# Decoder layer (scan, attention, experts) on one core: whole scan steps, unpadded queries and keys, maxima by one transpose

## The chip, the core and the metric

The kernel runs on one core of a Trainium2 chip. A core has five instruction queues that run beside each other: TensorE (PE: matrix products, with its own weight loads), VectorE (DVE), ScalarE (ACT), GpSimd (POOL) and SyncE (SP), which here issues every DMA. Each queue works in order, and an instruction that must wait holds up what stands behind it. Matrix products write to PSUM, which the kernel uses as eight banks of 512 numbers for each of 128 partitions; everything else lies in SBUF. The metric is the device time of one execution in microseconds; lower is better.

## The reference

32 sequences of 256 tokens and width 256 go through three blocks, each followed by a residual sum and a layer norm. All numbers are fp32.

```python
# 1: a selective scan (d_inner 512, 16 states), restarted every 64 tokens
xc, res = split(x @ W_in.T + b_in);  u = silu(causal_conv3(xc))
dlt, Bm, Cm = split(u @ W_x.T);      delta = softplus(dlt @ W_dt.T + b_dt)
carry = exp(delta * A) * carry + delta * Bm * u;   y = sum_n(carry * Cm)
x = layernorm(x + (y * silu(res)) @ W_out.T + b_out)
# 2: cross attention to ctx, 16 heads of 16
x = layernorm(x + softmax(q k^T / 4) v @ w_o.T + b_o)
# 3: 8 experts by position (32 tokens of each sequence), FF 704
x = layernorm(x + (silu(x w1) * (x w3)) w2)
```

## The kernel before

Everything is one program for 32 batches. The work is written as chains, Python generators that say which engine they need next and when they can go on; `in_order` always advances the chain that can start earliest (a chain's lag shifts its rank among those that want the same engine). The times that it goes by are constants in the source: `MM` for a matrix product, `EV`, `VE`, `GP` for evictions, 4.5 us (`LANDING`) for a DMA from issue to landing, and nothing for the issue itself. The order so found is fixed in the program; on the chip every queue keeps it.

The chains that matter here, with their lines in the profile:

- `pre(b)` (lines 346 to 466) projects the input, convolves, and makes `delta`, `u` and their product. It writes them to DRAM, and `load_step` (479) reads them back, spread over partitions, for one of 16 scan steps of a batch (two DMAs of 256 KB, four buffers).
- `decays` (506) makes the factors `da` of a step by four exponentials on ScalarE. `scan` (527) takes a step in two halves of 512 columns: a product `bu` into PSUM (L544), and the scan `h` (L563), both on VectorE. `weighted` (575) multiplies `h` by C on POOL (L580), and `sums` (583) adds over states on TensorE (L594) for four steps at a time, which frees four of the six buffers of `h`.
- `mixes` (651) is the output product, the residual and the layer norm of the scan block.
- `keys(b)` (619) projects keys and values of a batch. `attn(b)` (689) projects queries; both are written with each head padded from 16 to 32 rows, so that four heads fill 128 partitions (two products of two blocks each, L327). Scores are computed twice. First with queries on partitions (L715): VectorE takes each head's maximum (L731) into `mpad`, eight 128 x 128 transposes bring the maxima into the padding rows of the queries' layout (L739), and VectorE subtracts the result from `qT` (L742); a padding row of ones in `kT` does the rest. Then with keys on partitions: ScalarE takes the exponential of each head (L775), and TensorE multiplies by the values (L751). Scores always go by groups of four heads on four 32-row parts of TensorE, with a PSUM bank for each head.
- `finish(b)` (800) divides, projects and normalizes; it stores the result as `x2d`.
- `expert_unit` (947) takes one expert for two groups of four sequences; these units fill in between and remain at the end.

PSUM holds one bank for `bu`, one for `b_bc` (B spread over partitions) and a ring of six (`RING`) that all other products share through `take(n, rank, t)`, the lowest rank first. `keys`, `attn` and the next `keys` follow each other, since there is one set of keys and values; the scan of later batches runs beside them. All DMAs stand in SP's queue in the order of the chains. A DMA there also waits for the eighth one before it, since eight completion semaphores are used in turn.

Of the kernel before, what the change touches and what calls it, by code (L numbers as in the profile page):

```python
# [8 lines left out]
F32 = mybir.dt.float32  # L9
AF = mybir.ActivationFunctionType  # L10
ALU = mybir.AluOpType
# [19 lines left out]
RING = 6  # L31
# [64 lines left out]
def decoder_kernel(ctx: ExitStack, tc: tile.TileContext, a: dict, out: bass.AP):  # L96
# [58 lines left out]

    w_in = weight("w_in", D, 2 * DI)
# [29 lines left out]
    w_k = weight("w_k", D, NG * P)  # L186
    b_k = column("b_k", NG)
    w_v = weight("w_v", D, D)
    w_out = weight("w_out", DI, D)
    w_q = weight("w_q", D, NG * P)  # L190
    b_q = column("b_q", NG)
# [58 lines left out]
    mpad = keep.tile([P, 2, NG, P], F32, name="mpad")  # L250
    nc.gpsimd.memset(mpad, 0.0)
# [18 lines left out]

    def done(n, t):
        free.extend(n * [t])
# [13 lines left out]
    MM = 0.43  # L286
# [51 lines left out]
    xs_at, xps, dds, sress, bcds, ygs, spread, silus = {}, {}, {}, {}, {}, {}, {}, []  # L338
# [7 lines left out]
    def pre(b):  # L346
# [51 lines left out]
        u = unit1.tile([P, NDC, L], F32, tag="u", name=f"u_{b}")  # L398
        for c2 in range(2):
            t = biased(u, AF.Silu, conv_b, pss[c2], c2)  # L400
            done(1, t)
        nc.scalar.activation(sres, sres, AF.Silu)
# [4 lines left out]
        exps()  # L407
        yield from take(1, 3, t)
# [36 lines left out]
        for h in range(2):  # L445
            cc = slice(2 * h, 2 * h + 2)

            lost = unit1.tile([P, 2, L], F32, tag="xT", name=f"lost_{b}")
            nc.gpsimd.tensor_scalar(lost, e[:, cc], 1.0, -1.0, op0=ALU.add, op1=ALU.add)
            nc.gpsimd.tensor_tensor(lost, e[:, cc], lost, ALU.subtract)  # L450
            nc.gpsimd.tensor_tensor(z[:, cc], z[:, cc], lost, ALU.add)
            yield spend("POOL", 3 * GP[2]), "POOL" if h == 0 else "ACT"
# [13 lines left out]
        spread[b] = t + 3.0  # L466

    def pres():
        for b in range(B):
            yield from pre(b)  # L470
        while silus:
            silus.pop(0)()
# [54 lines left out]
    def scan():  # L527
# [4 lines left out]
        for i in range(STEPS):  # L532
            b, k = divmod(i, NBLK)
            if i + AHEAD < STEPS:
                yield lambda: spread.get((i + AHEAD) // NBLK), "SP"
                load_step(i + AHEAD)
            yield max(lds_at[i], b_bcs[b][1], recurred.get(i - 1, 0.0) - 0.3 - MARGIN), "DVE"
            b_bc = b_bcs[b][0]
            for g in range(GB):

                if g:
                    yield t - 0.3 - MARGIN, "DVE"
                bu = ps_bu.tile([P, NQ, L], F32, tag="bu", name="bu")
                nc.vector.tensor_tensor(  # L544
                    bu, loads[i][:, 1, g].unsqueeze(1).to_broadcast([P, NQ, L]), b_bc, ALU.mult
                )
                t = spend("DVE", 0.66)
                if g == GB - 1:
                    del loads[i]
                    if k == NBLK - 1 and b + 1 < B:  # L550
                        yield t, "PE"
                        spread_b(b + 1)
                t -= 0.3 + MARGIN
                if g == 0:
                    yield lambda: (
                        max(t, decayed[i], min(h_free)) if i in decayed and h_free else None
                    ), "DVE"
                    h_free.sort()
                    del h_free[0]
                    h = hs[i] = hp.tile([P, GB, NQ, L], F32, tag="h", name="h")  # L560
                else:
                    yield t, "DVE"
                nc.vector.tensor_tensor_scan(  # L563
                    h[:, g].rearrange("p q t -> p (q t)"),
                    das_of[i][:, g].rearrange("p q t -> p (q t)"),
                    bu.rearrange("p q t -> p (q t)"),
                    0.0,
                    op0=ALU.mult,
                    op1=ALU.add,
                )  # L570
                t = spend("DVE", 1.17)
            del das_of[i]
            recurred[i] = t
# [9 lines left out]
    def sums():  # L583


        for i in range(NJ - 1, STEPS, NJ):
# [16 lines left out]
            t = spend("PE", GB * NQ * MM + 0.3)  # L603
# [14 lines left out]

    def keys():

        for b in range(B):
# [4 lines left out]
            kT = unit1.tile([P, NG, L], F32, tag="kT", name=f"kT_{b}")  # L626
            for g2 in range(2):
                yield from take(1, 4, t0)
                ps, t = product(
                    "ps_qk",  # L630
                    lambda j: [
                        w_k[:, k, (2 * g2 + j) * P : (2 * g2 + j + 1) * P] for k in range(2)
                    ],
                    lambda j: [ctxT[:, k, :] for k in range(2)],
                )
                yield t, "ACT"
                t = biased(kT, AF.Identity, b_k, ps, g2)
                done(1, t)
# [10 lines left out]
            kts[b] = kT, t  # L649
# [39 lines left out]
    def attn(b):  # L689
# [3 lines left out]
        qT = unit1.tile([P, NG, L], F32, tag="qT", name=f"qT_{b}")  # L693
        for g2 in range(2):
            yield from take(1, 2, tx)
            ps, t = product(
                "ps_qk",
                lambda j: [w_q[:, k, (2 * g2 + j) * P : (2 * g2 + j + 1) * P] for k in range(2)],
# [471 lines left out]
```

## Time and profile before

| | |
|---|---|
| median of 3 runs | 3283.39 us (3279.27 to 3285.63) |
| profiled execution | 3283.71 us, span 3282.0 us, granted clock 0.897 |
| TensorE busy | 2697.9 us (82%) |
| VectorE busy | 2584.0 us (79%) |
| ScalarE, POOL busy | 1970.8 us (60%), 1857.3 us (57%) |
| DMA, mean | 139 GB/s, 47.8% of the engines' time |
| scan steps | 512, from 119 us on |

A group row of the profile names the line, the engine, the operation, output and inputs, shapes and count; behind the bar stand the busy time and the mean duration in ns, and then how long the engine had been idle before such instructions, with the instruction that ended most of it. An fp32 matrix product counts twice there, as two passes. A timeline row gives start and duration in us and how many instructions were merged; a window row gives the busy time of each engine in one stretch. SP's rows are issues of DMAs; they are not counted as busy.

### The profile page before, as it was taken

What the parts mean: (1) busy time and instruction counts of PE and PEld (TensorE: products, weight loads), DVE (VectorE), ACT (ScalarE), POOL (GpSimd) and SP (SyncE); (2) the same over time, 40 slices, a digit from 0 to 9 for tenths busy, and PEclk for the clock granted to TensorE, in tenths of its full rate; (3) what the DMA queues carried; (4) which work ended last, traced back from release to release, by engine and by line L of the source; (5) the groups of instructions that cost most, each with busy time, mean ns of one, the idle gap of its engine ahead of it and who ended that gap; (6) DMA issues with size and microseconds to landing.
All of it is one profiled execution on the core that took longest, in us unless ns stands there. A gap on an engine that the chain in (4) does not pass through costs nothing.

```text
span 3282.0 us, 52502 instructions
## 1 busy us (share of the span) xinstructions
PE 2697.9 (82%) x18436; PEld 1907.2 (58%) x18436; DVE 2584.0 (79%) x3511; ACT 1970.8 (60%) x4211; POOL 1857.3 (57%) x1241
## 2 busy tenths in 40 slices
PE   2568787878888988888888898888788888898987
PEld 1345555556556666566555566556566556565776
DVE  0598989898988988888989878989878898884211
ACT  0556666666666766676666656766656666764411
POOL 1576666666766656665656556665656666642000
PEclk9678888888889899999998899899899889899998
DMA  3354444444445555444544544445445544454474
GB/s 89 110 149 115 139 120 138 126 138 127 132 129 151 158 145 147 140 134 133 154 137 138 145 140 147 137 137 140 128 142 148 148 139 137 130 152 132 130 225 140
DMA packets 310681, 455.00 MB, mean 139 GB/s; under 512 B 37969, under 2 KB 158033, under 8 KB 310417
## 3 DMA queue, kind: packets, MB, share of 16 engines
q1 hardware_dynamic: 310416, 451.64, 47.8%
q8 instruction: 146, 2.39, 0.3%
q14 instruction: 119, 0.97, 0.1%
HBM read 400.67 MB, written 50.86 MB: 138 GB/s over the span
## 4 chain that ended last, share of the span: by engine, by line
DVE 44%; PE 27%; POOL 8%; ACT 8%; DMA 6%; issue 5%; SPq 2%; DVEq 1%; ACTq 0%; POOLq 0%
DVE h L563 23%; DVE bu L544 12%; PE ps_h L978 7%; PE s L715 4%; DVE mpad L731 4%; POOL h L580 3%; PE ps_down L1058 3%; PE ps_in L327 3%; PE y L594 3%; PE ps_oT L751 2%; ACT da L519 2%; ACT es L775 2%; PE ps_conv L327 2%; DMA ld<-dd 1%; PE ps_qk L327 1%
## 5 line engine op out<-in xcount | busy, mean ns | idle before, releaser
L580 POOL TENSOR_TENSOR h<-h,c_bc 128x1024 f32<-128x1024 f32 x512 | 1207.8, 2360 | 935.0 <-DVE h L563 810.8
L563 DVE TENSOR_TENSOR_SCAN h<-da,bu 128x512 f32<-128x512 f32 x1024 | 1248.4, 1219 | 116.8 <-PE y L594 11.0
L519 ACT ACTIVATE da<-ld,a_neg 128x252 f32<-128x252 f32 x2048 | 889.9, 506 | 395.6 <-DVE h L563 289.8
L544 DVE TENSOR_TENSOR bu<-ld,b_bc 128x512 f32<-128x512 f32 x1024 | 709.6, 693 | 95.4 <-PE b_bc L503 68.1
L594 PE MATMUL y<-h,sel_y 128*32 128x256 f32 x4096 | 334.1, 440 | 85.6 <-POOL h L580 73.4
L731 DVE TENSOR_REDUCE mpad<-s 128x2 f32<-128x512 f32 x512 | 315.5, 681 | 111.3 <-PE s L715 110.8
L775 ACT ACTIVATE es<-s 128x512 f32<-128x512 f32 x512 | 263.9, 601 | 191.6 <-PE ps_oT L751 144.9
L978 PE MATMUL ps_h<-x2T,w 128*128 128x256 f32 (+3 forms) x1440 | 331.0, 377 | 41.3 <-ACT x2T L966 36.2
L715 PE MATMUL s<-kT,qT 32*128 32x256 f32 x2048 | 248.9, 475 | 101.9 <-DVE mpad L731 63.3
L978 PEld LDWEIGHTS ps_h<-x2T,w 128*128 128x128 f32 (+1 forms) x1440 | 241.5, 193 | 110.7 <-ACT x2T L966 40.3
L594 PEld LDWEIGHTS y<-h,sel_y 128*32 128x32 f32 x4096 | 150.3, 124 | 253.8 <-POOL h L580 119.6
L327 PE MATMUL ps_in<-xT,w_in 128*128 128x256 f32 x1024 | 268.9, 415 | 13.5 <-ACT xT L352 12.0
L715 PEld LDWEIGHTS s<-kT,qT 32*128 32x128 f32 x2048 | 155.4, 218 | 189.2 <-DVE mpad L731 98.8
L327 PEld LDWEIGHTS ps_in<-xT,w_in 128*128 128x128 f32 x1024 | 205.5, 208 | 68.9 <-issue 12.8
L715 PE MATMUL s<-qT,kT 32*128 32x256 f32 x2048 | 180.1, 438 | 39.4 <-DVE qT L742 23.4
L301 POOL TENSOR_SCALAR ln_rstd<-ln_mv 128x2 f32<-128x2 f32 x96 | 22.0, 230 | 309.6 <-DVE ln_mv L298 305.0
L327 PE MATMUL ps_conv<-xpad,taps 128*128 128x256 f32 x768 | 182.6, 388 | 0.0
L751 PE MATMUL ps_oT<-es,v 128*32 128x256 f32 x2048 | 149.1, 410 | 40.6 <-DVE h L1040 13.1
L1058 PE MATMUL ps_down<-w,h 128*128 128x256 f32 (+1 forms) x624 | 164.2, 409 | 16.4 <-DVE h L1040 7.5
L715 PEld LDWEIGHTS s<-qT,kT 32*128 32x128 f32 x2048 | 112.4, 202 | 96.1 <-issue 25.6
L327 PEld LDWEIGHTS ps_conv<-xpad,taps 128*128 128x128 f32 x768 | 146.5, 194 | 25.0 <-issue 3.1
L327 PE MATMUL ps_out<-w_out,yg 128*128 128x256 f32 x512 | 133.2, 419 | 28.5 <-ACT es L775 20.9
(124 smaller groups left out, 3701.4 us busy)
## 6 DMA issues: line engine op xcount, KB each, us to landing
ld<-dd SPq DMA_DIRECT2D x1024, 256.0 KB
w<-in_w SPq DMA_DIRECT2D x120, 352.0 KB
x<-in_x SPq DMA_DIRECT2D x64, 256.0 KB
dd<-delta SPq DMA_DIRECT2D x32, 512.0 KB
dd<-u SPq DMA_DIRECT2D x32, 512.0 KB
w13y<-in_w SPq DMA_DIRECT2D x40, 352.0 KB
w<-in_w SPq DMA_DIRECT2D x30, 384.0 KB
ctxT<-in_ctxT SPq DMA_DIRECT2D x32, 256.0 KB
```

Of the source, the lines that this page charges most:

```text
L327: nc.tensor.matmul(ps[:, j, :], l, r, start=(k == 0), stop=(k == len(terms) - 1))
L519: nc.scalar.activation(da[:, g, q].rearrange("p (k t) -> p k t", t=CHUNK)[:, :, 1:], loads[i][:, 0, g].rearrange("p (k t) -> p k t", t=CHU ...
L544: nc.vector.tensor_tensor(bu, loads[i][:, 1, g].unsqueeze(1).to_broadcast([P, NQ, L]), b_bc, ALU.mult)
L563: nc.vector.tensor_tensor_scan(h[:, g].rearrange("p q t -> p (q t)"), das_of[i][:, g].rearrange("p q t -> p (q t)"), bu.rearrange("p q t - ...
L580: nc.gpsimd.tensor_tensor(hs[i], hs[i], c_bc, ALU.mult)
L594: nc.tensor.matmul(y[32 * j : 32 * j + 32, :], sel_y[:, g, :], hs[i - NJ + 1 + j][:, g, q, :], start=(g == 0 and q == 0), stop=(g == GB - ...
L715: nc.tensor.matmul(ss[j][:, t, :], left[r : r + 32, g, t * P : (t + 1) * P], right[r : r + 32, g, :], start=True, stop=True,)
L731: nc.vector.tensor_reduce(mpad[:, :, g, 32 * j + DK], s, AX.X, ALU.max)
L751: nc.tensor.matmul(oT[32 * j : 32 * j + 32, :], v[:, k, 4 * g + j, :], ess[j][:, k, :], start=(k == 0), stop=(k == 1), tile_position=(0, 3 ...
L775: nc.scalar.activation(es, s, AF.Exp, scale=1.0 / DK**0.5)
L978: nc.tensor.matmul(ps[:m, i, :], w_tiles[u, which, e][k][:, f * P : f * P + m], right, start=(k == 0), stop=(k == 1),)
L1058: nc.tensor.matmul(po[:, j, :], h[i // m_in][:m, i % m_in, cols], w_tiles[u, "w2", e][f // 3][:m, f % 3, :], start=(i == terms[0]), stop=( ...
```

## The change

- A scan step is one product of 1024 columns into two PSUM banks and one scan of 1024. The ring of shared banks falls from six to five.
- Queries and keys are projected without padding: one product of two blocks instead of two. Each is evicted to a flat tile, from which 16 DMAs bring the heads to the old places (32 rows apart) in `qT` and `kT`, which are now fixed tiles. `kT` is set to one once. The weights are packed while loading (two DMAs each, pieces of 64 bytes), the biases by 16 DMAs each.
- Maxima are gathered in `tops`, 32 columns; one transpose makes 32 rows of them, ScalarE copies these with the sign turned, and 32 DMAs of one row each write them into the 17th row of each head in `qT`. The second scores contract 17 rows, the first 16.
- Scores go by two heads, or by four where `more` finds two further banks free.
- `u` has two buffers, and the second half of `pre` is a chain of its own (`sizes`, `steps`); `lost` works on quarters; the value of `MM` and some of the planner's constants change.

```diff
-RING = 6
+RING = 5
...
+    def heads(n):
+        w = wp.tile([P, 2, D], F32, name="w_" + n)
+        src = a["w_" + n].rearrange("(k p) (h c) -> p k h c", p=P, c=32)
+        for k in range(2):
+            dst = w[:, k].rearrange("p (h c) -> p h c", c=DK)
+            nc.sync.dma_start(dst, src[:, k, :, :DK])
...
+            nc.sync.dma_start(bias[r : r + DK, h // 8 : h // 8 + 1], src)
...
-    mpad = keep.tile([P, 2, NG, P], F32, name="mpad")
-    nc.gpsimd.memset(mpad, 0.0)
+    kT = keep.tile([P, NG, L], F32, name="kT")
+    nc.gpsimd.memset(kT, 1.0)
+    qT = keep.tile([P, NG, L], F32, name="qT")
+    tops = keep.tile([P, 2, H], F32, name="tops")
...
+    def more(n):
+        if sum(t <= clock.now for t in free) < n or len(asking) > 1 and min(asking) < 2:
+            return 0
+        free.sort()
+        del free[:n]
+        return n
...
-    MM = 0.43
+    MM = 0.47
...
-        u = unit1.tile([P, NDC, L], F32, tag="u", name=f"u_{b}")
+        u = unit2.tile([P, NDC, L], F32, tag="u", name=f"u_{b}")
...
-        for h in range(2):
-            cc = slice(2 * h, 2 * h + 2)
-            lost = unit1.tile([P, 2, L], F32, tag="xT", name=f"lost_{b}")
...
+        for c in range(NDC):
+            lost = unit1.tile([P, L], F32, tag="lost", name=f"lost_{b}")
...
-            for g in range(GB):
...
-                bu = ps_bu.tile([P, NQ, L], F32, tag="bu", name="bu")
...
+            bu = ps_bu.tile([P, GB, NQ, L], F32, tag="bu", name="bu")
+            nc.vector.tensor_tensor(
+                bu,
+                loads[i][:, 1].unsqueeze(2).to_broadcast([P, GB, NQ, L]),
+                b_bc.unsqueeze(1).to_broadcast([P, GB, NQ, L]),
+                ALU.mult,
+            )
...
+            nc.vector.tensor_tensor_scan(
+                h.rearrange("p g q t -> p (g q t)"),
+                das_of.pop(i).rearrange("p g q t -> p (g q t)"),
+                bu.rearrange("p g q t -> p (g q t)"),
+                0.0, op0=ALU.mult, op1=ALU.add,
+            )
...
+    def spread_heads(dst, flat):
+        for g in range(NG):
+            for j in range(4):
+                h = 4 * g + j
+                r = DK * (h % 8)
+                nc.sync.dma_start(dst[32 * j : 32 * j + DK, g, :], flat[r : r + DK, h // 8, :])
...
-        for g in range(NG):
-            yield from take(4, 2, tq)
-            ss, ts = scores(g, qT, kT)
-            for j, s in enumerate(ss):
+        h = 0
+        while h < H:
+            yield from take(2, 2, tq)
+            n = 2 + more(2 if h % 4 == 0 else 0)
+            ss, ts = scores(range(h, h + n), qT, kT, DK)
+            for s in ss:
                 yield ts, "DVE"
-                nc.vector.tensor_reduce(mpad[:, :, g, 32 * j + DK], s, AX.X, ALU.max)
+                nc.vector.tensor_reduce(tops[:, :, h], s, AX.X, ALU.max)
...
-                    nc.tensor.transpose(ps[:, j, n, :], mpad[:, n, 2 * g2 + j, :], ident)
...
-            nc.vector.tensor_tensor(q2, q2, ps.rearrange("p j t n -> p j (t n)"), ALU.subtract)
...
+        ps = bank("ps_m")[: 2 * H, :P]
+        nc.tensor.transpose(ps, tops.rearrange("p t h -> p (t h)"), ident)
...
+        nc.scalar.activation(rows, ps, AF.Identity, scale=-1.0)
...
+        for t in range(2):
+            for g in range(NG):
+                for j in range(4):
+                    h = t * H + 4 * g + j
+                    r = 32 * j + DK
+                    nc.sync.dma_start(qT[r : r + 1, g, t * P : (t + 1) * P], rows[h : h + 1, :])
+        tq = clock.now + LANDING
```

## The prediction

> **What bounds the kernel now.** I read the page's shares first, then the windows by stage, then single rows of the timeline. One execution took 3283.7 us around a span of 3282.0; the median of the runs shown is 3283.4, so sums against the span need 1.7 us more.
>
> ```profile
> PE 2697.9 (82%) x18436; PEld 1907.2 (58%) x18436; DVE 2584.0 (79%) x3511; ACT 1970.8 (60%) x4211; POOL 1857.3 (57%) x1241
> ...
> 0.00:120.00 120.00, 41.17 (x162) 34.05 (x163) 4.99 (x25) 22.90 (x41) 22.36 (x34) 0.93 0.32 86
> ...
> 1500.00:2100.00 600.00, 512.01 (x3628) 356.92 (x3621) 521.34 (x699) 398.85 (x864) 373.38 (x240) 0.91 0.49 139
> ...
> 3000.00:3282.00 282.00, 248.59 (x1524) 200.37 (x1524) 61.03 (x135) 77.24 (x143) 19.00 (x53) 0.93 0.50 156
> ```
>
> Each window row gives the stretch and its length, then the busy time of TensorE, its weight loads, VectorE, ScalarE and POOL, the granted clock and the DMA's share. In the middle stage TensorE works 512 of 600 us and VectorE 521. With some 0.1 us between neighbours on VectorE (699 instructions) that is 95% of the stage: VectorE sets the pace, TensorE stands close behind. The first scores of batch 0 start at 212 us, those of batch 31 at 3025: 90.7 us a batch. TensorE idles 3282 - 2698 = 584 us, of it 79 before 120 us and 33 after 3000. The granted clock is 0.91 to 0.93 whether TensorE is busy a third of the stretch (the start) or nearly nine tenths (the end), so I reckon with no change of it.
>
> ```profile
> L563 DVE TENSOR_TENSOR_SCAN h<-da,bu 128x512 f32<-128x512 f32 x1024 | 1248.4, 1219 | 116.8 <-PE y L594 11.0
> L544 DVE TENSOR_TENSOR bu<-ld,b_bc 128x512 f32<-128x512 f32 x1024 | 709.6, 693 | 95.4 <-PE b_bc L503 68.1
> ...
> L742 DVE TENSOR_TENSOR qT<-qT,ps_m 128x512 f32<-128x512 f32 x64 | 41.9, 674 | 5.1 <-PE ps_m L739 5.0
> L739 PE MATMUL ps_m<-ident,mpad 128*128 128x128 f32 x256 | 45.2, 302 | 22.0 <-DVE mpad L731 22.0
> L327 PE MATMUL ps_qk<-x1T,w_q 128*128 128x256 f32 x512 | 126.1, 391 | 0.0
> L327 PE MATMUL ps_qk<-ctxT,w_k 128*128 128x256 f32 x512 | 125.3, 389 | 7.2 <-DMA ctxT<-in_ctxT 4.7 <-DVE yg L610 2.5
> ...
> 1524.97 1.15 PE L715 MATMUL s<-qT,kT 32*128 32x256 f32 x16
> ```
>
> These are the work that changes: scan and product, the subtraction and transposes of the maxima, the projections, and (last line) one group of scores, four heads in 1.15 us.
>
> The resource that the page hardly shows is SP's queue:
>
> ```profile
> 7.89 40.98 SPq L181 DMA_DIRECT2D a_neg<-in_a_log  x64
> ...
> 50.44 0.26 ACT L183 ACTIVATE a_neg<-a_neg 128x64 f32<-128x64 f32 x1 [48.37 <-DMA a_neg<-in_a_log]
> ...
> L422 SPq DMA_DIRECT2D bcd<-xp x32: 335/524/1106, 91.8 to 2836.6; - x32
> L485 SPq DMA_DIRECT2D ld<-dd x1024: 513/554/1889, 111.6 to 2962.7; - x171
> ```
>
> Whatever its size (16 rows in L422, 256 KB in L485), an issue holds SP about 0.54 us; 64 tiny ones took 0.64 each. The last of these ended at 48.87 and ScalarE, which needed it, started at 50.44: 1.6 us to landing.
>
> **The change, part by part.**
>
> Whole scan steps. L1040's product with a PSUM operand takes 413 ns for 256 elements and 687 for 512: 274 per 256, 139 fixed. So 1024 cost 1.235 us instead of 2 x 0.693. The scan shows one size: 2.30 if its fixed part is the same 139, 2.44 if nothing is fixed; I take 2.30. In an undisturbed stretch a half step recurs every 2.07 us (product starts at 118.99, 121.07, 123.12), so 0.16 of it is gaps, then paid once. A step falls from 4.13 to 3.69 us: 225 us over 512 steps (154 with the dearer scan). The subtraction's 42 us go too. VectorE has 267 us less, 8.3 a batch. That is no gain unless TensorE can follow.
>
> TensorE's work. The projections halve: -126. One transpose of 32 columns a batch for eight: -45 + 32 x 0.3 = -36. Scores: the built program holds 77 groups of four heads and 358 of two where there were 256 of four, because the ring has five banks. 16 passes on four row groups are four slots (1.15 us); two heads are eight passes on two row groups, again four slots. So 179 groups are added at about 1.0 us (some overlap with neighbours): +179. Bounds: 0 if two heads cost half, +206 at the full 1.15. Work after: 2698 - 126 - 36 + 179 = 2715. The saved padding is spent again.
> The Trainium skill ("TensorEngine Tiling (Array Packing)", Key Properties) says that a change of tiling mode drains TensorE, which speaks against more, smaller groups; in the trace the weight load at 1521.24, after scores, shows 0.33 us of "issue" before it. By the rule, 179 groups x 2 changes x 0.33 would be an estimated 118 us more.
>
> The maxima's new path. Before, VectorE subtracted them. Now: transpose, a ScalarE copy of 128 columns (between 0.26 for 64 columns in L183 and 0.47 for 256 in L416: 0.35), then 32 SP issues of one row each, ordered by half and then by head. The first score group needs both halves of its heads, hence the 17th issue: 0.1 + 0.35 + 0.1 + 17 x 0.54 + 1.6 = 11.3 us (8.4 at 0.37 each, the low end of L422; 18 if 20 issues at 0.64 are needed and landing takes the 4.7 us of the longest wait of L519 for a load). The planner adds 4.5 us and nothing for SP. In the built order the first score group follows the transpose directly in 19 of 32 batches; the others have 0.7 to 5 us between, 28 in all. What is queued behind: sums of y, on which the release of four of six h buffers hangs, so VectorE runs dry after two more steps (7.4 us). Dead time: 32 x 11.3 - 28 = 334 (241 to 548). The same place cost 22.0 (L739) + 23.4 (first scores after L742) = 45.
>
> Spreading queries and keys: 16 issues each. Their first group needs four: 4 x 0.54 + 1.6 = 3.8 us, and between projection and scores most batches have 10 to 25 us of TensorE work. I cost it at nothing on TensorE; without that cover it is 32 x 3.8 = 122.
>
> SP's total: 64 issues x 0.54 = 35 us more a batch, beside some 55 x 0.54 = 30 us. It fits in 90, but loads stand behind bursts. Four load buffers are four steps, 14.8 us; a burst of 32 plus landing plus the exponentials (1.7) is 20.6. VectorE can run dry for 5.8 us; that falls in the same dead stretch, so I don't add it (+186 if it did not).
>
> Start: 34 more issues stand before the first load of x, 17 to 22 us, and the queries' and keys' weights now come in 64-byte pieces: 8192 against 128 pieces in each of the 64 small transfers at 0.64 us, up to 41. I take +30 (17 to 60).
>
> Two buffers of u and separate size computation, `lost` in quarters (12 instructions for 6), 4 fewer ScalarE evictions: POOL and ScalarE are 57% and 60% busy. Nothing, bounded by 20 us either way.
>
> Sum, on TensorE's queue: work 2715; idle at the start 79 + 30, at the end 33; dead 334; and the remaining waits. Before, these were 584 - 79 - 33 - 45 = 427, of which waits for POOL's h are 86 (L594), b_bc 38 and scores for reductions 102 (L715): upstream engines get ahead during the dead time, so I drop them and keep 200. The bounds are 0 and 427; the bank that the ring loses works towards the upper one, since scores, sums and projections all wait for banks, and the wait of scores for reductions (102) is the row that it would lengthen. 2715 + 109 + 33 + 334 + 200 = 3391, and 1.7 around it: **3393 us**, 3.3% slower.
> Another rule of the skill, to coalesce many small transfers ("DMA: Bandwidth & Descriptors", Rules for kernel authors), speaks against 64 pieces a batch too; that page puts a fixed 2.0 us on a transfer, which for the 1.6 measured here would give an estimated 13 us more.
>
> **Rivals.**
> Faster: the other waits collapse, since all that stands behind the dead stretch is ready when it ends, and VectorE's 267 us count. The break-even is remaining waits under 92 us (183 if the dead stretch is the short 8.4). With 0 to 92: 3191 to 3283; I name 3200. For: TensorE's waits are mostly on VectorE and POOL. Against: waits inside attention (L751 41, L978 41, L327 after exponentials 28) don't depend on the scan.
> Much slower: late loads and dead stretches don't coincide, and the waits remain: 3393 + 186 = 3579. For: in 12 late batches 43 to 46 issues stand between two load steps (25 us). Against: there the scan waits for its buffers anyhow.
> The change does what its words say: two-head groups are cheap (half): 3393 - 179 = 3214. The four slots of 1.15 us speak against it.
>
> **Numbers.** Slower as summed 0.55, much slower 0.16, faster by waits or cheap groups 0.26, unchanged 0.03. The runs spread by 0.2% (3279.3 to 3285.6), which is what can be told from no change. The range reaches into the faster cases down to 3190 and the slow one up to 3600; the likeliest case's own is 3300 to 3500.
>
> **What would show it.** Right: in nearly every batch TensorE idles 9 to 14 us between the transpose of maxima and the next scores, released by a DMA; about 435 score groups; a scan row near 2.30 us, a product near 1.24; VectorE's share falls below 75%. Wrong: row issues well under 0.4 us, TensorE above 82% busy, or the scores' busy time not rising.

## The result

The changed kernel takes 4075.1 us (median, 4064.6 to 4080.6), the kernel before 3282.8 in the same runs: a ratio of 1.241, with a 95% interval of 1.238 to 1.244. The prediction was 3393 (3190 to 3600). The sign is right, and the loss is seven times as large: 792 us, not 110. The profiled execution has a span of 4069.2 us and 1.7 us around it.

The lines of the page after that answer to those shown of before: shares by engine, granted clock, the chain that ended last by engine, then the groups (busy time and mean ns behind the bar, then idle time ahead of them and who ended it).

```profile
PE 3015.8 (74%) x17700; PEld 2056.3 (51%) x17700; DVE 2404.7 (59%) x2423; ACT 1937.1 (48%) x4135; POOL 1888.8 (46%) x1433
...
PEclk9777877777778877778878777887777887778878
...
PE 38%; SPq 18%; DVE 14%; DMA 11%; ACT 8%; issue 6%; POOL 4%; DVEq 0%; ACTq 0%; POOLq 0%
...
L592 DVE TENSOR_TENSOR_SCAN h<-da,bu 128x1024 f32<-128x1024 f32 x512 | 1169.2, 2284 | 121.1 <-PE y L621 65.0
L554 ACT ACTIVATE da<-ld,a_neg 128x252 f32<-128x252 f32 x2048 | 863.3, 499 | 762.9 <-DMA ld<-dd 488.9
L576 DVE TENSOR_TENSOR bu<-ld,b_bc 128x1024 f32<-128x1024 f32 x512 | 627.0, 1225 | 201.2 <-DMA ld<-dd 107.0
L751 PE MATMUL s<-qT,kT 17*128 17x256 f32 x2048 | 394.4, 541 | 411.6 <-DMA qT<-rows 368.6
```

The rows of before that answer to the second, the third and (from the list of waits) the fifth of these lines:

```profile
PEclk9678888888889899999998899899899889899998
...
DVE 44%; PE 27%; POOL 8%; ACT 8%; DMA 6%; issue 5%; SPq 2%; DVEq 1%; ACTq 0%; POOLq 0%
```

```profile
ACT da L519 <- DMA ld<-dd: 97.1, 71, 4.7
```

After the change no engine is busy for more than three quarters of the span. The chain held 44% VectorE and 2% SyncE's queue before; now SyncE's queue is 18% of it. ScalarE's wait for the loads of the scan steps, 97 us before, is 489. TensorE's wait for the rows of maxima is 369, close to what was predicted. The granted clock fell from 0.897 to 0.793: TensorE's 318 us of extra busy time are about the same work at a slower clock (by the span's mean clock, 2698 x 0.897 = 2420 us at full clock before, 3016 x 0.793 = 2392 after).

By stage: the first scan starts at 139 us instead of 120, the last one at 3621 instead of 2982, and from there to the end it takes 448 us instead of 300. So 620 of the 787 us that the span grew lie in the scan stage (108.8 us a batch, before 89.4), 148 in the tail and 19 at the start.

What happens in the scan stage shows in 30 us of the timeline (start, duration, queue, instruction; in brackets the idle time before it and its releaser):

```profile
1432.59 0.39 PE L774 MATMUL ps_m<-ident,tops 128*32 128x128 f32 x1 [3.10 <-DVE tops L768]
...
1433.73 1.16 SPq L520 DMA_DIRECT2D ld<-dd  x2
...
1434.98 20.54 SPq L786 DMA_DIRECT2D qT<-rows  x32
...
1437.45 2.29 DVE L592 TENSOR_TENSOR_SCAN h<-da,bu 128x1024 f32<-128x1024 f32 x1
...
1441.13 2.29 DVE L592 TENSOR_TENSOR_SCAN h<-da,bu 128x1024 f32<-128x1024 f32 x1
...
1446.90 3.89 PE L751 MATMUL s<-qT,kT 17*128 17x256 f32 x16 [13.92 <-DMA qT<-rows]
...
1454.50 0.42 DVE L637 TENSOR_TENSOR yg<-y,sres 128x256 f32<-128x256 f32 x1 [11.08 <-PE y L621]
...
1455.62 5.35 SPq L520 DMA_DIRECT2D ld<-dd  x8
...
1456.20 2.29 DVE L592 TENSOR_TENSOR_SCAN h<-da,bu 128x1024 f32<-128x1024 f32 x1
...
1458.94 1.69 ACT L554 ACTIVATE da<-ld,a_neg 128x252 f32<-128x252 f32 x4 [6.87 <-DMA ld<-dd]
```

SyncE issues 32 rows from 1434.98 to 1455.52. TensorE waits 13.9 us for them, with the sum of y behind the scores in its queue, and VectorE for that sum. But the loads of the next scan steps stand in SyncE's queue behind the same 32 issues: the first goes out at 1455.62 and ScalarE can use it at 1458.94. Two waits end at nearly the same time.

### The profile page after: what moved, and what is told of

Its sections match the earlier page's. It is cut to its first block, busy times and chain, and to the rows that moved or that the text cites. A ratio compares the mean times of both kernels' runs of the same rounds, so it can differ in the third digit from the quotient of the medians.

```text
span 4069.2 us, 52673 instructions
## 1 busy us (share of the span) xinstructions
PE 3015.8 (74%) x17700; PEld 2056.3 (51%) x17700; DVE 2404.7 (59%) x2423; ACT 1937.1 (48%) x4135; POOL 1888.8 (46%) x1433
## 4 chain that ended last, share of the span: by engine, by line
PE 38%; SPq 18%; DVE 14%; DMA 11%; ACT 8%; issue 6%; POOL 4%; DVEq 0%; ACTq 0%; POOLq 0%
SPq L786 12%; PE s L751 8%; DVE h L592 7%; PE ps_h L1024 6%; DMA ld<-dd 5%; PE ps_down L1104 4%; ACT da L554 4%; PE ps_in L351 4%; PE y L621 4%; SPq L652 3%; DVE bu L576 3%; PE ps_oT L794 2%; DVE tops L768 2%; PE ps_conv L351 2%; PE ps_qk L351 2%
## 5 line engine op out<-in xcount | busy, mean ns | idle before, releaser
L592 DVE TENSOR_TENSOR_SCAN h<-da,bu 128x1024 f32<-128x1024 f32 x512 | 1169.2, 2284 | 121.1 <-PE y L621 65.0
L576 DVE TENSOR_TENSOR bu<-ld,b_bc 128x1024 f32<-128x1024 f32 x512 | 627.0, 1225 | 201.2 <-DMA ld<-dd 107.0
L751 PE MATMUL s<-qT,kT 17*128 17x256 f32 x2048 | 394.4, 541 | 411.6 <-DMA qT<-rows 368.6
L751 PEld LDWEIGHTS s<-qT,kT 17*128 17x128 f32 x2048 | 252.2, 251 | 540.0 <-issue 421.0
L768 DVE TENSOR_REDUCE tops<-s 128x2 f32<-128x512 f32 x512 | 323.6, 682 | 241.4 <-PE s L751 240.6
L751 PE MATMUL s<-kT,qT 16*128 16x256 f32 x2048 | 325.1, 465 | 128.0 <-DMA kT<-k_flat 31.4
L1024 PE MATMUL ps_h<-x2T,w 128*128 128x256 f32 (+1 forms) x1488 | 389.7, 413 | 39.8 <-DMA w<-in_w 9.5
L1024 PEld LDWEIGHTS ps_h<-x2T,w 128*128 128x128 f32 x1488 | 273.3, 211 | 143.8 <-issue 63.6
L751 PEld LDWEIGHTS s<-kT,qT 16*128 16x128 f32 x2048 | 199.0, 215 | 233.8 <-issue 81.9
L478 POOL TENSOR_SCALAR lost<-ez 128x256 f32<-128x256 f32 x128 | 137.6, 1075 | 108.8 <-ACT ez L473 104.9
```

Of the source, the lines that this page charges most:

```text
L576: nc.vector.tensor_tensor(bu, loads[i][:, 1].unsqueeze(2).to_broadcast([P, GB, NQ, L]), b_bc.unsqueeze(1).to_broadcast([P, GB, NQ, L]), AL ...
L592: nc.vector.tensor_tensor_scan(h.rearrange("p g q t -> p (g q t)"), das_of.pop(i).rearrange("p g q t -> p (g q t)"), bu.rearrange("p g q t ...
L751: nc.tensor.matmul(s[:, t, :], left[r : r + n, g, t * P : (t + 1) * P], right[r : r + n, g, :], start=True, stop=True,)
L768: nc.vector.tensor_reduce(tops[:, :, h], s, AX.X, ALU.max)
L1024: nc.tensor.matmul(ps[:m, i, :], w_tiles[u, which, e][k][:, f * P : f * P + m], right, start=(k == 0), stop=(k == 1),)
```

## The experiments

The theories: A, SyncE's queue, whose short issues hold up the loads of the scan. B, TensorE's clock, which halves after the dead stretch. C, the price of five banks and of scores by two heads. An account of SyncE goes with A: the issues' median is 587 ns for a row of 0.5 KB, for 16 KB of a spread and for a load of 256 KB alike (the source rows of the three lines: minimum, median and maximum in ns):

```profile
L786 SPq DMA_DIRECT2D qT<-rows x1024: 497/587/1547, 265.0 to 3932.3; - x171
...
L652 SPq DMA_DIRECT2D kT<-k_flat x512: 507/587/1591, 92.1 to 3887.2; - x171
...
L520 SPq DMA_DIRECT2D ld<-dd x1024: 513/587/2181, 132.1 to 3602.2; - x171
```

Taking the waits that the profile lists for SyncE from the span leaves 984 us of issuing before (3282 - 2298) and 2326 after (4069 - 1743): 42 us a batch for 64 small DMAs. SyncE is not the bound (57% of the span), so what it costs had to be tried. In the table, a kernel without an interval was run once; runs of one kernel differ by up to 0.6%.

| kernel | small DMAs a batch | us | ratio to before (95%) |
|---|---|---|---|
| five banks alone (`e4_ring`) | 0 | 3314 | 1.007 to 1.013 |
| five banks, whole steps (`e5_steps`) | 0 | 3264 | 0.990 to 0.997 |
| the same, four heads always (`e18_fours`) | 0 | 3383 | 1.026 to 1.034 |
| `e5_steps`, rows by 4 DMAs (`e16_rows_only`) | 4 | 3331 | 1.010 to 1.018 |
| the same, a fifth load buffer (`e20_rows_ahead`) | 4 | 3326 | 1.007 to 1.018 |
| merged (`e1_merged`) | 20 | 3463 | 1.051 to 1.059 |
| merged, idle products (`e11_merged_warm`) | 20 | 3454 | 1.045 to 1.059 |
| merged, issued by ScalarE (`e13_merged_act`) | 20 | 3631 | 1.102 to 1.110 |
| rows alone merged (`e15_rows`) | 36 | 3686 | |
| before, unused DMAs (`e3_spare`) | 64 | 3895 | |
| `e5_steps`, unused DMAs (`e21_steps_spare`) | 64 | 3987 | |
| changed kernel | 64 | 4075 | 1.238 to 1.244 |
| rows by heads (`e2_head_order`) | 64 | 4056 | |
| idle products behind the copy (`e10_warm`) | 64 | 4094 | |
| DMAs paced (`e9_paced`) | 64 | 4152 | |
| idle products ahead of the copy (`e7_warm`) | 64 | 4375 | |
| issued by ScalarE (`e12_act`) | 64 | 4428 | |

**Unused DMAs on the kernel before.**

```diff
+    def spare(src):            # behind keys and behind queries
+        for g in range(NG):
+            for j in range(4):
+                r = 32 * j
+                nc.sync.dma_start(scr[r : r + DK, g, :], src[r : r + DK, g, :128])
...
+        yield tq, "SP"             # behind the maxima
+        ...
+                    nc.sync.dma_start(scr[r : r + 1, g, 64 * t : 64 * t + 64],
+                                      qT[r : r + 1, g, t * P : t * P + 64])
```

> The kernel before with 64 small DMAs more for a batch, issued where the change issues its own (16 behind the keys, 16 behind the queries, 32 behind the maxima) and into a scratch tile that nobody reads. The output is the same. It has SyncE's 37 us more for a batch, but nobody waits for the rows. Theory A, late loads: the step's loads and the loads of x1 come late as in the changed kernel, ScalarE's waits for loads rise from 97 us towards 490: 3450 to 3700. If only the dead stretch of TensorE (with or without the clock) costs: 3280 to 3340. Theory C says 3280 to 3300.

3895 us, 612 more than before and above the upper end that theory A gave. Nobody waits for what these DMAs bring (half as many bytes each as those of the change, at the same median of 587 ns for the pieces of queries and keys). The waits of this kernel (microseconds in total, times, longest):

```profile
POOL h L582 <- DVE h L565: 1036.2, 323, 21.6
ACT da L521 <- DMA ld<-dd: 973.5, 161, 21.2
...
DVE bu L546 <- DMA ld<-dd: 215.6, 27, 15.6
```

ScalarE waits 973 us for loads, the longest 21.2 us, about as long as a burst of 32 issues. The clock is 0.836 here, though TensorE's work is untouched: a lower clock comes with late loads.

**Merged DMAs.** Four rows' DMAs of eight rows each and two groups of heads in one spread: 20 instead of 64.

```diff
-        for t in range(2):
-            for g in range(NG):
-                for j in range(4):
-                    h = t * H + 4 * g + j
-                    r = 32 * j + DK
-                    nc.sync.dma_start(qT[r : r + 1, g, t * P : (t + 1) * P], rows[h : h + 1, :])
+        for j in range(4):
+            r = 32 * j + DK
+            nc.sync.dma_start(qT[r : r + 1, :, :], rows[8 * j : 8 * j + 8, :])
...
+        for odd in range(2):
+            for j in range(4):
+                r = DK * (4 * odd + j)
+                nc.sync.dma_start(dst[32 * j : 32 * j + DK, odd::2, :], flat[r : r + DK, :, :])
```

> The changed kernel with 20 small DMAs for a batch in place of 64: each spread of queries and keys by 8 DMAs (two groups of heads at once), the rows of maxima by 4 (eight rows each, to one partition); tops is ordered so that the rows of one partition are neighbours. All else stays, and the output is the same. Theory A (SyncE's issues, 0.6 us each, keep TensorE waiting for the rows and make the loads of the scan late): 44 issues of 0.6 us are 26 us of SyncE less for a batch, the dead stretch falls from some 12.5 us to 4 or 5, and 32 x 8 = 250 us go, together with about half of the 490 us that ScalarE waits for loads: 3600 to 3830. Theory B (the clock of TensorE halves because of the dead stretch): the gain is larger, since the 26 us at half speed behind the stretch go as well if it is short enough: granted clock 0.87 to 0.90 instead of 0.79, 3300 to 3600. Theory C (five banks and scores by two heads): above 3950, since neither changes here.

3463: 612 us less than the changed kernel, at a clock of 0.843. The same bytes move; the merged issues take 591 and 657 ns (medians). Theory C fails. The time is in B's range and better than A's, but the clock is below the 0.87 that B asked for; the runs with idle products part them.

**Rows in the order of the heads.**

```diff
-        for t in range(2):
-            for g in range(NG):
-                for j in range(4):
+        for g in range(NG):
+            for j in range(4):
+                for t in range(2):
```

> The changed kernel with its 32 rows of maxima issued in the order of the heads (both halves of a head one after the other), not all first halves ahead of all second ones. The output is the same and SyncE has as much to issue. The first four heads are complete after 8 issues instead of 20, so TensorE's first second scores can start some 12 x 0.6 = 7 us earlier. Theory A, the part of it that is the dead stretch: 32 x 7 = 224 us less where the rest is covered, 3850. The part of it that is late loads: no change, 4050 to 4080. Theory B: with a dead stretch of 5 or 6 us instead of 12.5 the half clock comes later or not at all, 3600 to 3800 at a clock of 0.85 or more. Theory C: 4050 to 4080.

4056, 19 us less than the changed kernel's median in one run, which hardly tells a difference. The waits of this kernel:

```profile
ACT da L554 <- DMA ld<-dd: 722.5, 90, 19.9
...
DVE bu L576 <- DMA ld<-dd: 288.1, 31, 54.9
...
PE s L751 <- DMA qT<-rows: 100.1, 41, 5.7
```

TensorE's wait for the rows falls from 369 us to 100, as intended. ScalarE's wait for loads rises from 489 to 723. The time that was taken from the one wait went to the other, which ended at the same place.

**Idle products for the clock.** 23 matrix products behind the transpose keep TensorE busy. In the first form they stood ahead of ScalarE's copy of the maxima, which then waited for them.

```diff
         nc.tensor.transpose(ps, tops.rearrange("p t h -> p (t h)"), ident)
+        for _ in range(WARM):
+            nc.tensor.matmul(whole[:, L:], ident, taps[:, :2, :], start=True, stop=True)
```

> The changed kernel with 23 matrix products more behind the transpose of the maxima, into a part of its bank that nobody reads: idle work for TensorE in the dead stretch, about 10 us at full clock. The output is the same; nothing else moves. Theory B (TensorE's clock halves because it stands idle): the 26 us at half clock behind the stretch go, which is about 13 us of 32 batches, 400 us at most and some 200 if only half of it lay on the path: 3650 to 3900, granted clock 0.87 to 0.9, and the first second scores take 1.9 us instead of 3.9. If the clock has another cause: 4060 to 4150 at 0.79, the products being paid where the rows come earlier than they end.

4375: the copy waited 389 us for the products, so the rows left some 12 us later in each batch, and 300 us of that showed. It tells nothing of the clock. With the same lines behind the copy:

> The changed kernel with 23 matrix products more for TensorE in the dead stretch, now behind ScalarE's copy of the maxima, so that the copy doesn't wait for them (in the first trial with such products it did, for 389 us). The output is the same. Theory B: granted clock 0.85 to 0.9, the first second scores of a batch at full speed, 3700 to 3950. If late loads keep TensorE without work in any case: the clock rises, and the time stays within 50 us of 4075, or above by up to 23 x 0.43 x 32 = 316 us where the products come in the way.

4094, 19 us more, again within what runs differ by. The window at half clock of the changed kernel, the same window of this one, and its page:

```profile
1560.50:1587.00 26.50, 19.58 (x113) 10.27 (x114) 12.11 (x10) 11.22 (x26) 8.27 (x4) 0.50 0.61 153
```

```profile
1560.50:1587.00 26.50, 14.13 (x109) 7.55 (x112) 11.95 (x11) 10.92 (x25) 7.57 (x4) 0.73 0.62 147
```

```profile
PE 3332.7 (81%) x19172; PEld 2320.9 (57%) x19172; DVE 2404.9 (59%) x2423; ACT 1935.8 (47%) x4135; POOL 1889.2 (46%) x1433
...
PEclk9788877887788888888888888987887887879878
```

The clock rises to 0.832, short of the 0.85 that theory B asked for, and in this window to 0.73; the first second scores in it take 2.9 us instead of 3.9. TensorE's idle time ahead of such scores falls from 412 us to 92, but only because the idle products fill it: these scores start at 1561.23 us, in the changed kernel at 1560.51. Behind them TensorE waits longer for ScalarE's exponentials (the changed kernel's row first):

```profile
1579.10 3.64 PE L621 MATMUL y<-h,sel_y 128*32 128x256 f32 x32 [6.91 <-ACT es L819]
```

```profile
1580.31 3.64 PE L622 MATMUL y<-h,sel_y 128*32 128x256 f32 x32 [11.69 <-ACT es L823]
```

So the kernel is no faster. Theory B fails as a cause, as far as the clock was raised. In the merged kernel, where TensorE is busy 83% of the span, 8 such products:

> The merged kernel (20 DMAs for a batch, 3463) with 8 idle matrix products behind ScalarE's copy of the maxima, 3.2 us of TensorE's time while the rows are on their way. The output is the same. TensorE is busy for 83 per cent of this kernel's span, so its clock (0.843, against 0.909 with whole steps and five banks alone) could matter here more than in the changed kernel. Theory B: clock above 0.87, 3360 to 3440. If the clock only follows the waits: 3460 to 3510, the products adding up to 32 x 1.5 us.

3454 at 0.867. The clock rose by 0.024, and the interval against the kernel before (1.045 to 1.059) holds the merged kernel's 1.055: no change that can be told. Neither outcome that was written down for it came: the clock just missed 0.87, and the time lies between the two.

**The banks and whole steps, without any small DMA.** First the ring of five and the scores by two or four heads, on the kernel before; then whole steps as well, that is, the scan of the change in place of the loop over halves.

```diff
-RING = 6
+RING = 5
...
-            yield from take(4, 2, tq)
-            ss, ts = scores(g, qT, kT)
+            yield from take(2, 2, tq)
+            n = 2 + more(2 if h % 4 == 0 else 0)
+            ss, ts = scores(range(h, h + n), qT, kT, 32)
```

> The kernel before with one part of the change alone: five shared banks in place of six, and scores by two heads, or by four where two further banks are free. Half scan steps, padded queries and keys, the eight transposes and all DMAs are as before; the output is the same. Theory C (banks and groups cost): the 181 us that the merged kernel is still behind the kernel before lie here, 3420 to 3500, with a granted clock near 0.85. If they come from the 20 DMAs that are left or from the rows' wait: 3270 to 3330, the extra groups being worth at most 179 us by the price of the prediction.

3314: 31 us slower than before, so theory C's cost is small.

> The same kernel (five banks, scores by two or four heads, all else as before) with whole scan steps as well: one product of 1024 columns into two banks and one scan of 1024. The output is the same. It is the change without its DMAs and its unpadded queries and keys. Theory A: VectorE gains 14 us of work for each batch and SyncE nothing to do more, so it is faster than the one with five banks alone by some 50 to 200 us, and near or below the kernel before: 3150 to 3350. Theory C: no faster than the merged kernel, 3400 to 3500.

3264: 50 us less than with five banks alone, and the fastest kernel of all, though by only 0.3 to 1.0% against the kernel before. Its page shows TensorE in front, at a clock of 0.909, with VectorE well behind:

```profile
PE 2838.4 (87%) x18436; PEld 1997.5 (61%) x18436; DVE 2437.4 (75%) x2487; ACT 1977.2 (61%) x4231; POOL 1860.2 (57%) x1241
```

ScalarE waits 58.6 us for loads, and the scan stage takes 86.7 us a batch (from 120 to 2895 us). So 811 us separate the changed kernel from this one. Is the loss of the ring the groups of two? With fours only, in both places:

```diff
-            yield from take(2, 2, tq)
-            n = 2 + more(2 if h % 4 == 0 else 0)
+            yield from take(4, 2, tq)
+            n = 4
```

> Whole scan steps and five banks (3264), with scores by four heads always, as in the kernel before, and never by two. The output is the same. If the groups of two cost what the prediction put on them (179 us for 358 of them, or a part of it): 3100 to 3240. If waiting for four of five banks costs as much as the groups of two: 3250 to 3350.

3383, 119 us slower. The groups of two do cost TensorE work (2838 x 0.909 = 2580 us at full clock against 2774 x 0.885 = 2455), but waiting until four of five banks are free costs more. Against the kernel before, with its six banks, the work of `e4_ring` is 176 us more (2859 x 0.908 = 2596 against 2420).

**Which of the DMAs.** Rows merged as above, spreads left at 32:

> The changed kernel with the rows of the maxima alone merged: 4 DMAs of eight rows in place of 32, and the 32 DMAs that spread queries and keys as they are: 36 for a batch. The output is the same. If each small DMA costs the same wherever it stands (the line through 64 DMAs at 4075 and 20 at 3463, 13.9 us for each of a batch): 3463 + 16 x 13.9 = 3686. If the rows, which the attention of the batch waits for, are what costs: 3463 to 3520. If the spreads are: 3950 to 4050.

3686, on the line through 64 and 20: each small DMA of a batch costs 13.9 us over the 32 batches, 0.43 us apiece, for the 28 of the rows that are gone here (390 us) as for the 16 of the spreads that are gone in the merged kernel (222 us). With rows alone, on padded queries and keys (no spreads, the row of ones in the keys as before):

```diff
-                    nc.tensor.transpose(ps[:, j, n, :], mpad[:, n, 2 * g2 + j, :], ident)
...
+        nc.tensor.transpose(ps, tops.rearrange("p h t -> p (h t)"), ident)
...
+        for j in range(4):
+            r = 32 * j + DK
+            nc.sync.dma_start(qT[r : r + 1, :, :], rows[8 * j : 8 * j + 8, :])
```

> Whole scan steps and five banks (3264) with the maxima by one transpose as well, its rows brought into the padding rows of the queries by 4 merged DMAs; queries and keys stay padded, so nothing is spread. The output is the same. It has 4 small DMAs for a batch. By the same 13.9 us for each: 3264 + 56 = 3320, less the 36 us of transposes and 44 us of VectorE's subtractions where these lie on the path: 3240 to 3340. If the wait of attention for the rows' landing, some 4 us a batch, is what costs: 3264 + 128 = 3390.

3331, 67 us more than without: four DMAs at 16.7, near the slope, but the next run says that this is not for the same reason. A fifth buffer for the loads:

```diff
-AHEAD = 3
+AHEAD = 4
```

> The kernel with whole steps, five banks and four merged rows, with a fifth buffer for the loads of the scan steps, which are fetched four steps ahead and not three. The output is the same. If late loads are what the small DMAs cost: faster than without the fifth buffer by up to the 56 us of its four DMAs, and below 3264: 3180 to 3260. If it is the landing of the rows: no change against the run without, within 15 us.

3326: ScalarE's wait for loads falls from 49 us to 12 and the time stays. The cost of four DMAs is thus not late loads; TensorE's waits for rows (84 and 70 us) are the rows of the wait view that fit it, but no run took them away.

**Occupation or waiting.** The 64 unused DMAs of the first experiment, with the same lines, on whole steps and five banks:

> The kernel with whole steps, five banks and padded queries and keys (3264) with the same 64 unused DMAs for a batch that cost the kernel before 612 us. The output is the same. If SyncE's issues cost the same here, 3264 + 612 = 3876, and what the changed kernel has above that, some 200 us, is its own waiting for what the DMAs bring (rows, queries, keys). If whole steps, which take a load at once and not in two halves, suffer more from late loads: 3950 to 4100, and the waiting is worth nothing.

3987, 723 us more than without them and 111 more than the first case expected, inside the range of the second. The waits for loads, without these DMAs (`e5_steps`) and with them:

```profile
ACT da L527 <- DMA ld<-dd: 58.6, 38, 10.7
```

```profile
ACT da L529 <- DMA ld<-dd: 701.5, 109, 20.9
...
DVE bu L551 <- DMA ld<-dd: 371.3, 31, 30.4
```

So of the 811 us nine tenths appear when SyncE is merely occupied. SyncE's own waits for what these DMAs send are 117 us in all, so it is mostly their issues that occupy it. That whole steps suffer more from late loads than half steps, as the second case has it, is not shown: ScalarE and VectorE wait 1073 us for loads here and 1189 in `e3_spare`. The rest of the 811 is mixed: the changed kernel has less projection work, waits for its rows and spreads, and has the other parts of the change (two buffers of `u`, a split `pre`, other constants), which no run took alone.

**Another queue, another order.** ScalarE issues the 64, or the merged 20, right behind the instruction that makes their source.

```diff
-                nc.sync.dma_start(dst[32 * j : 32 * j + DK, g, :], flat[r : r + DK, h // 8, :])
+                nc.scalar.dma_start(dst[32 * j : 32 * j + DK, g, :], flat[r : r + DK, h // 8, :])
...
-        tq = clock.now + LANDING
+        tq = spend("ACT", 32 * ISSUE) + LANDING
```

> The changed kernel with its 64 small DMAs of a batch issued by ScalarE's queue, right behind the instruction that makes their source, and not by SyncE's; the order of the work counts 0.6 us of ScalarE for each. The output is the same. If it is SyncE's queue that costs (its loads for the scan stand behind the bursts): the late loads go, ScalarE's wait for loads falls below 150 us, but ScalarE gets 64 x 0.6 = 38 us a batch on top of its 60, 1230 us in all, which makes it the engine with most to do, about 3150 us: 3400 to 3700. If the 64 transfers themselves cost, whoever issues them: 3950 to 4150.

> The merged kernel (20 DMAs for a batch) with these 20 issued by ScalarE's queue. The output is the same. ScalarE gets 20 x 0.6 = 12 us a batch on top of its 61, and SyncE has no more to issue than in the kernel before. If SyncE's queue is what the merged kernel still pays for, the 199 us that it is behind the kernel with whole steps and five banks alone (3264) go, and the 126 us of projections and 36 us of transposes that TensorE is spared show: 3120 to 3290. If the 20 transfers cost by their landing (the chain of attention waits for three of them in a row for each batch): 3350 to 3500.

4428 and 3631: both slower than from SyncE, by 353 and 167 us, and above every case written down. For the 64, on ScalarE's queue:

```profile
1588.53 0.27 ACT L778 ACTIVATE rows<-ps_m 32x128 f32<-32x128 f32 x1 [4.05 <-PE ps_m L775]
1588.83 20.60 ACTq L787 DMA_DIRECT2D qT<-rows  x32
1609.47 6.44 ACT L555 ACTIVATE da<-ld,a_neg 128x252 f32<-128x252 f32 x16 [20.67 <-DMA qT<-rows]
```

An issue costs the queue 0.64 us there as well, and the exponentials of four scan steps stood behind the burst. The late loads are gone, as expected (ScalarE waits 7 us for them), though the same 64 transfers run: it is SyncE's queue that makes loads late. The scan is late all the same. ScalarE is busy only 44 to 53% of the span; what counts is where its instructions stand, not the sum that my expectation was made of. The Trainium skill ("DMA: Bandwidth & Descriptors", Rules for kernel authors) says that spreading DMAs over several queues saves issue time only; in these two runs it moved that time to a queue where it cost more.

The last trial left the count and the queue and let other chains' DMAs in between:

```diff
                 nc.sync.dma_start(dst[32 * j : 32 * j + DK, g, :], flat[r : r + DK, h // 8, :])
+            yield clock.now + 2.4, "SP"
```

> The changed kernel with the same 64 DMAs, but handed to the order of the work four at a time, 2.4 us apart, so that other chains' DMAs (the loads of the scan steps above all) can take their place in SyncE's queue between them, and so that the order of the work counts on the rows only when the last four are issued. The output is the same. Theory A in the form that bursts keep the loads back: the loads are late no longer, ScalarE's wait for them falls from 490 us towards 100, TensorE has other work in the stretch: 3400 to 3700. If SyncE's total (some 110 issues of 0.6 us for a batch, 66 us) is what costs, or the chain of attention that waits for the rows: 3900 to 4100.

4152, 77 us slower. The longest wait of ScalarE for a load falls from 19.8 to 11.7 us, but there are 109 of them instead of 86, 426 us in all; SyncE issues for as long (4150 - 1809 = 2341 us). The bursts as such are not the cause. TensorE's wait for rows fell to 47 us, and again that bought nothing. Which wait replaced it in this order stays open. This order counts 2.4 us for four issues in the chain that makes them, but not as time of SyncE's queue; an order that counts every issue there was not run, so how much of the loss such an order could take back is open too.

## Why the prediction was wrong

| step of the prediction | said | measured |
|---|---|---|
| scan, product (mean us) | 2.30, 1.235 | 2.284, 1.225 |
| TensorE's work | 2715 at an unchanged clock | 2392 at full clock = 2666 at 0.897; 3016 at 0.793 |
| start | +30 | +19 |
| end | no change | +148 (448 us for 300) |
| dead wait for rows | 334 | 369 |
| spreads of queries and keys | nothing | 222 us for 16 of the 32 |
| late loads | not added (+186 in a rival) | within the 723 us of an occupied SyncE; their own share was not parted |

**Right:** the durations of whole steps, SyncE's 0.54 us for an issue of any size (587 ns), the dead wait and its place. VectorE is below 75%, but at 59% of a span far longer than predicted this says little. Whole steps gain little (50 us), with TensorE in front: from 1500 to 2100 us of `e5_steps` it works 546 of 600 us, VectorE 487.

**The step that failed** is SyncE's total. It let 35 us more a batch pass with "It fits in 90", and of the late loads it said "that falls in the same dead stretch, so I don't add it". It took the rows' burst for the only one and the dead wait for what carries the cost. In fact the order is the other way round: occupying SyncE costs 723 us with nobody waiting for what its 64 DMAs bring (`e21_steps_spare`), and taking most of the dead wait away changed the time by 19 us down (`e2_head_order`, 100 us of wait left) and 77 us up (`e9_paced`, 47 left). The 334 was well measured and on a path beside which another, equally long one ran. Two waits that start at one burst end together, so the price of the burst is neither wait but the burst. For the same reason the upstream engines did not get ahead in the dead time, by which the sum had dropped 227 us of other waits: ScalarE's loads stood behind the same issues, and it waited 489 us for them.

The spreads at nothing failed for the same reason: TensorE's 10 to 25 us of other work cover the wait for the data, not the 20 us for which the loads behind them in SyncE's queue stand still. By the slope of 13.9 us the 32 spreads are 445 us and the 32 rows 445; that carries the line on to a changed kernel without any, which was not run.

The groups of two were sized about right as TensorE work (179 taken; +176 us at full clock for `e4_ring` against the kernel before) and wrong as a loss: with five banks they cost 31 us in all, and five banks without them are slower still.

That the clock would stay was wrong (0.793 for 0.897), and lifting it part of the way (0.832) changed no time. The three windows that it was read from, at 0.91 to 0.93, passed over the slices from 82 to 246 us of the same page, at 0.6 and 0.7, and those at 0.8 that follow.

The rival "much slower by late loads" named the mechanism and priced one burst a batch at 5.8 us; there are three, and the scan stage takes 22 us a batch more than in `e5_steps` (108.8 against 86.7). "Remaining waits 200 of 427" has no counterpart left to be compared with. The tail's 148 us were not in any case of mine: in the changed kernel three batches of attention remain when the scan ends (384 passes of scores behind 3621 us; before, 128 behind 2982), and experts wait for them. `e5_steps`, without the DMAs, also has 359 passes and 366 us left behind its scan, so part of it is not theirs.

Four readings of the prediction are off without moving its result: 521 us and 699 gaps of 0.1 us make 98.5% of the stage, not 95%; of the 86 us ahead of L594 73 are waits for POOL, and of the 102 ahead of L715 63 are waits for the reductions; and the estimate of 13 us from a fixed 2.0 us a transfer uses a figure that the Trainium skill ("DMA: Bandwidth & Descriptors", Anatomy of one DMA) fits to DMAs issued by GpSimd, while SyncE issues these.

## What to carry to other kernels

Count what a change adds to a queue that works in order, and then look at what stands behind each burst: in `e21_steps_spare` a queue occupied for 42 us more a batch cost 23 us a batch although it was busy only 58% of the time and nobody waited for what the added DMAs brought. Merge small DMAs before anything else, since an issue took the same 0.6 us for 0.5 KB as for 256 KB; another order, pacing, or a busy compute queue as the issuer bought nothing. And when a wait is priced, ask which other wait ends at the same moment: in `e2_head_order` taking one of two away gained next to nothing.

## What had not been expected of the hardware

TensorE's granted clock was 0.50 for 26.5 us behind a stretch of 12.5 us in which TensorE had worked 1.9 us, although it was recorded busy for 19.6 of these 26.5 us, the first 11.7 without a break:

```profile
1560.50:1572.20 11.70, 11.69 (x56) 6.46 (x56) 3.62 (x4) 2.07 (x4) 4.17 (x2) 0.50 0.19 47
```

The Trainium skill ("TensorE: Matmul & The Clock Gate", What's actually happening) has half rate end after some 3.4 us of sustained work; this window shows a longer return. What counts as work for the clock, no run here shows.

The 3.9 us of the group of scores behind the wait are not the clock's alone. In the group at 1446.90 us the first products of its four heads start at 1446.90, 1447.51, 1448.12 and 1448.75 us, about one issue of SyncE apart: each waits for the rows of its own head. A later group of four heads at the same half clock (1568.24 us) takes 2.1 us, and one at full clock (1690.03 us) 1.15. In `e3_spare`, where TensorE has the same work as before, the clock was 0.836.
